# An FFN on the high parts of its weights, with a general path behind an If, on one Trainium2 core

## The chip, the cores and the metric

The kernel runs on one core of one Trainium2 chip. The metric is the device time of one execution in microseconds; less is better. Before the change the median of three runs is 2959.37 us (2954.0 to 2959.81).

## What is computed

The input x has 2 batches of 2048 tokens with 256 features, in float32. Cut to what matters:

```python
x = x + _layernorm(attn(_layernorm(x), Wq, bq, Wk, bk, Wv, bv, Wo, bo, gamma, beta))
x = x + _layernorm(ffn(_layernorm(x), w_gate, w_up, w_down))

# attn: 16 heads of 64, softmax over 2048 keys, then
#   y = x + attn_out; layer norm of y with eps 1e-3, times gamma, plus beta
# ffn: weights are int32 from -127 to 127, times SCALE = 1/127; HIDDEN is 768
gate = jnp.einsum('bsd,hd->bsh', x, wg)
up = jnp.einsum('bsd,hd->bsh', x, wu)
h = jax.nn.silu(gate) * up
return jnp.einsum('bsh,dh->bsd', h, wd)
```

## The kernel before

Products that must be more precise than the fast float32r format are made of two parts. A value is split into a high part (a cast to float32r) and a low part (what is left). A product then takes three matmuls: high by high, high by low, low by high.

**The attention** is 64 units (batch, pair of heads, block of 512 queries). It takes the first 2720 us. TensorE makes maxima of scores, scores and the product with V; ScalarE makes exponentials; VectorE and GpSimd add them up. Beside it, short jobs run in pieces: `piece` in `prep_jobs` (L328) loads 128x256 of integer weights, casts and transposes them, splits them into high and low parts and writes both to HBM; 18 of these jobs cover the three weights. `load_ffn` (L361) reads them back in the last units. `ahead_job` is the first of four `own_job`s (L393).

**The FFN** is written out by hand for PE, DVE, ACT and POOL; SP's order is left to the scheduler. Eight chunks of 512 tokens, six blocks of 128 hidden features each, make 48 slots, numbered 0 to 47 here. In each slot, `gate_up` (L968) issues on PE two accumulations of six matmuls, gp and up (128x512 each, two buffers each); on ACT the Silu of gp (`sg`, L984); on DVE `hf`, up times sg (L986); on ACT the cast to the high part of hT (L988); on POOL its low part (L989). After gate_up every job that is running makes one step, up to its next `yield`:

- `end_job` of the chunk before (L1037), started in a chunk's second slot: four output tiles (`down`, L992, 18 matmuls of 128x256 each; one tile, one tile, two tiles), their statistics, the reciprocal root (`ln_rstd`, L99: 13 small steps on DVE), then scale, residual add on POOL and output.
- `own_job`, for the four chunks of the second batch: three layer norms in a row on the attention's result, each with statistics (L96, L97), the 13 small steps, and two applies on ACT per step (L137), with adds and products on POOL (L416).
- `x_out` (L955): transposes of a chunk's normalized rows and their split.
- `last_units` (L1082): what is left of the attention.

Each engine works through its instructions in order: what stands in front of sg or hf on ACT or DVE delays it. Where each own_job starts is given by slot numbers:

```python
OWN_AT = {2: OWN + 1, 14: OWN + 2, 24: OWN + 3}
```

The intermediates of the 13 small steps lie in a PSUM bank (`chain`, L430). `finish` (L1053) makes the last chunk's four tiles and the final outputs.

Of the kernel before, what the change touches and what calls it, by code (L numbers as in the profile page):

```python
# [8 lines left out]
F32 = mybir.dt.float32  # L9
# [7 lines left out]
P = 128  # L17
# [8 lines left out]


@with_exitstack
def kernel(
    ctx: ExitStack,  # L30
# [15 lines left out]
    out: bass.AP,  # L46
):
    nc = tc.nc
    B, S, D = x.shape
# [27 lines left out]
    xT_dram = dram.tile([B, NC, P, 2, DC, TB], F32, name="xT_dram")  # L77
    wg_dram = dram.tile([P, 2, DC, HID], F32, name="wg_dram")
    wu_dram = dram.tile([P, 2, DC, HID], F32, name="wu_dram")
    wd_dram = dram.tile([P, 2, HC, D], F32, name="wd_dram")  # L80


    mvx = [const.tile([P, NT, 2], F32, name=f"mvx{b}") for b in range(B)]
    rsx = [const.tile([P, NT], F32, name=f"rsx{b}") for b in range(B)]
    nbx = [const.tile([P, NT], F32, name=f"nbx{b}") for b in range(B)]

    small["pool"] = st
# [10 lines left out]

    def ln_rstd(rs, nb, mv, n, eps, eng=None, bank=None):  # L99

        eng = eng or nc.vector

        def temp(k, name, dtype=F32):
            if bank is not None and name not in ("ng", "ny"):
                return bank[:, k * n : (k + 1) * n]
            return small["pool"].tile([P, n], dtype, tag=f"{name}{n}", name=name, bufs=2)

        v = temp(0, "nv")  # L110
        eng.tensor_scalar(v, mv[:, :, 1], eps, None, ALU.add)
        g = temp(1, "ng", I32)
        eng.tensor_scalar(g, v.bitcast(I32), -0.5, 1597463007.0, ALU.mult, ALU.add)

        def stt(out, a, s, b, op0):

            if eng is nc.vector:
                eng.scalar_tensor_tensor(out, a, s, b, op0, ALU.mult)
            else:
                eng.tensor_scalar(a, a, s, None, op0)  # L120
                eng.tensor_tensor(out, a, b, ALU.mult)

        h = temp(2, "nh")
        eng.tensor_scalar(h, v, -0.5, None, ALU.mult)
        y = g.bitcast(F32)
        for i in range(3):
            t = temp(3, "nt")
            eng.tensor_tensor(t, h, y, ALU.mult)
            t2 = temp(4, "nu")
            eng.tensor_tensor(t2, t, y, ALU.mult)  # L130
            d = rs if i == 2 else temp(5, "ny")
            stt(d, t2, 1.5, y, ALU.add)
            y = d
        stt(nb, mv[:, :, 0], -1.0, rs, ALU.mult)

# [192 lines left out]
    def prep_jobs():  # L328
        jobs = []

        def piece(w, dst, o, i0):
            src = hd.tile([P, TT, D], F32, tag="hx", name="wi")[:, 0, :].bitcast(I32)
            nc.sync.dma_start(out=src, in_=w[o * P : (o + 1) * P, i0 * P : (i0 + 2) * P])
            yield "R"
            f = hd.tile([P, TT, D], F32, tag="hy", name="wf")[:, 0, :]
            nc.scalar.copy(f, src)
            yield "F"
            ps = double()[:, 0, :]
            for i in range(2):
                nc.tensor.transpose(ps[:, i * P : (i + 1) * P], f[:, i * P : (i + 1) * P], ident)  # L340
            t = hd.tile([P, TT, D], F32, tag="ht", name="wt")[:, :2, :].bitcast(F32R)
            split(t, ps[:, : 2 * P])
            for k in range(2):
                nc.sync.dma_start(
                    out=dst[:, k, i0 : i0 + 2, o * P : (o + 1) * P],
                    in_=f32(t[:, k, :]).rearrange("p (i n) -> p i n", i=2),
                )

        for w, dst, no, ni in (
            (w_gate, wg_dram, HC, DC),  # L350
            (w_up, wu_dram, HC, DC),
            (w_down, wd_dram, DC, HC),
        ):
            for o in range(no):
                for i0 in range(0, ni, 2):
                    jobs.append(piece(w, dst, o, i0))
        return jobs
# [3 lines left out]
    def load_ffn(which):  # L361

        if which < 2:
            full = aw.tile([P, DC, S], F32R, tag=("xh", "xl")[which], name=f"fw{which}")
            full = full.rearrange("p c n -> p (c n)")
            n = 2 * DC * HID
            t = full[:, :n].rearrange("p (w c n) -> p w c n", w=2, c=DC)
            for w in range(2):
                for dc in range(DC):
                    nc.sync.dma_start(  # L370
                        out=f32(t[:, w, dc, :]), in_=(wg_dram, wu_dram)[which][:, w, dc, :]
                    )
                    yield None

            x0T[which] = full[:, n : n + DC * TB].rearrange("p (c n) -> p c n", c=DC)
            nc.sync.dma_start(out=f32(x0T[which]), in_=xT_dram[0, 0, :, which])
        else:
            i = 2 * (which - 2)
            t = kp.tile([P, 2, 2, D], F32R, tag="T1", name=f"fw{which}")
            for w in range(2):  # L380
                nc.sync.dma_start(out=f32(t[:, w]), in_=wd_dram[:, w, i : i + 2, :])
                yield None
        fwt[which] = t
# [9 lines left out]
    def own_job(ch):  # L393
# [5 lines left out]
        def norm(dst, src, eps, *then):  # L399
            pool = small["pool"]  # L400
            mv = pool.tile([P, TT, 2], F32, tag="mvh4", name="mvh")
            for n in range(0, TT, 2):
                ln_stats([src[:, n + i, :] for i in range(2)], mv, n)
                if n == 0:
                    yield
            rs = pool.tile([P, TT], F32, tag="rsh4", name="rsh")
            nb = pool.tile([P, TT], F32, tag="nbh4", name="nbh")
            ln_rstd(rs, nb, mv, TT, eps, *chain())
            for n in range(0, TT, 2):
# [19 lines left out]

    def chain():  # L430

        if "chain" in banks:
            return nc.vector, banks["chain"].tile([P, 512], F32, tag="c", name="chain")
        return nc.gpsimd, None
# [493 lines left out]
    banks["pool"] = ctx.enter_context(tc.tile_pool(name="ps_m", bufs=1, space=PSUM))  # L928
    banks["chain"] = ctx.enter_context(tc.tile_pool(name="ps_c", bufs=1, space=PSUM))
    fs = ctx.enter_context(tc.tile_pool(name="fs", bufs=2))  # L930
# [37 lines left out]
    def gate_up(ch, hc):  # L968
        gp = ps_g.tile([P, TB], F32, tag="g", name="gp")
        up = ps_g.tile([P, TB], F32, tag="u", name="up")  # L970
        for ps, w in ((gp, fwt[0]), (up, fwt[1])):
            n = 0
            for dc in range(DC):
                for wi, xi in ((0, 0), (0, 1), (1, 0)):
                    nc.tensor.matmul(  # L975
                        ps,
                        w[:, wi, dc, hc * P : (hc + 1) * P],
                        xTs[ch][xi][:, dc, :],
                        start=n == 0,
                        stop=n == 5,  # L980
                    )
                    n += 1
# [9 lines left out]
    def down(ch, i, hcs=range(HC)):  # L992
# [7 lines left out]
        for hc in hcs:  # L1000
            for n, (hi, wi) in enumerate(((0, 0), (0, 1), (1, 0))):
                nc.tensor.matmul(  # L1002
                    fp_tile(ch, i),
                    hTs[ch, hc][:, hi, i * P : (i + 1) * P],
                    fwt[2 + hc // 2][:, wi, hc % 2, :],
                    start=hc == 0 and n == 0,
                    stop=hc == HC - 1 and n == 2,
                )
# [6 lines left out]
    def end_stats(ch, i, mv):  # L1015
        ln_stats([fp_tile(ch, i)], mv, i)

    def end_rstd(mv):
        rs = small["pool"].tile([P, TT], F32, tag="rso", name="rso")
        nb = small["pool"].tile([P, TT], F32, tag="nbo", name="nbo")  # L1020
        ln_rstd(rs, nb, mv, TT, LN_EPS, *chain())
        return rs, nb

# [13 lines left out]
    def end_job(ch):  # L1037

        mv, before = end_mv(), ()
        for tiles in ((0,), (1,), (2, 3), ()):  # L1040
# [4 lines left out]
            before = tiles  # L1045
            if not tiles:
                ready = end_rstd(mv)
            yield
        end_out(ch, 0, *ready, nc.gpsimd)
        yield  # L1050
        end_out(ch, 2, *ready, nc.gpsimd)

    def finish(ch):  # L1053
# [3 lines left out]
        def end(tiles, eng):  # L1057
# [5 lines left out]
            nb = small["pool"].tile([P, n], F32, tag=f"nbe{n}", name="nbe")  # L1063
            ln_rstd(rs, nb, mv[:, :n, :], n, LN_EPS, *chain())
            yield
# [16 lines left out]
    def last_units():  # L1082

        wo_half(units[-2], 1)
        yield
        ps = bank()
        sum_up(last, ps)
# [7 lines left out]
        wo_half(last, 0)  # L1095
        yield
        yield
        wo_half(last, 1)

# [5 lines left out]
    end = len(chunks) - 1  # L1105
    OWN_AT = {2: OWN + 1, 14: OWN + 2, 24: OWN + 3}
    with tc.manual_schedule(engines={EV.PE, EV.DVE, EV.Activation, EV.Pool}):
        ffn_load(0)
        ffn_load(1)
        for ch in range(len(chunks)):  # L1110
            for hc in range(HC):
                gate_up(ch, hc)
                n = len(slots)
                if n == 0:
                    jobs.append(last_units())
                if n in OWN_AT:
                    jobs.append(own_job(OWN_AT[n]))
                if ch > 0 and hc == 1:
                    jobs.insert(0, end_job(ch - 1))
                if hc == 1 and OWN <= ch + 1 < len(chunks):  # L1120
                    jobs.append(x_out(ch + 1))
                for j in list(jobs):
# [5 lines left out]
        for j in jobs:  # L1128
            drain(j)
        finish(end)  # L1130


# [45 lines left out]
```

## Time and profile before

| what | value |
|---|---|
| runs, median of three | 2959.37 us |
| the profiled execution | 2961.08 us, its span 2959.3 us |
| mean granted TensorE clock | 0.992 |
| first gate_up on PE | 2724.71 us |
| hf of slot 0, of slot 46, of slot 47 | 2729.27, 2938.18, 2942.39 us |
| down in 2740 to 2960 us, x576 | busy 74.0 us |
| last vector add | 2955.84 us |

In the profile's rows an instruction reads: line, engine, operation, output from inputs, shapes, count, busy time in us, mean length in ns, then the engine's idle time just before and what ended it. "PE" is TensorE's matmuls, "PEld" its weight loads, "DVE" VectorE, "ACT" ScalarE, "POOL" GpSimd, "SP" the engine that issues most DMAs. Lengths of matmuls overlap; their rate is read from the chain, where a group's total is given. All times are from the span's start.

### The profile page before, as it was taken

To read this page: it belongs to the slowest core of one execution; us is meant where nothing else is said; L and a number is where in the kernel's file an instruction comes from. 1 tells how busy PE (TensorE), PEld (TensorE's weight loads), DVE (VectorE), ACT (ScalarE), POOL (GpSimd) and SP (SyncE) were. 2 spreads that over 40 slices of the span, in tenths; PEclk is the share of its full clock that TensorE was granted. 3 is DMA by queue.
4 is the path that set the end of the run, shared out by engine and by line. 5 is a ranking of instruction groups with operands and counts; after the bars stand their busy time and mean duration, and the time that the engine had idled before them with its cause. 6 is when DMAs were issued, how large, how long until landed. Compare 5 with 4: busy or idle time off the path is not lost.

```text
span 2959.3 us, 48771 instructions
## 1 busy us (share of the span) xinstructions
PE 2876.9 (97%) x19492; PEld 1742.6 (59%) x19492; DVE 2102.9 (71%) x2701; ACT 1467.1 (50%) x1740; POOL 2444.7 (83%) x1399
## 2 busy tenths in 40 slices
PE   7999999999999999989999999999999999999998
PEld 5555565556555565555655655555655555555787
DVE  6776677777777777766677767777677767774653
ACT  4545454544445444554455545555455445554443
POOL 4999878888788878877799989998799889888453
PEclk9999999999999999999999999999999999999999
DMA  2000000000000001010000001000000000012000
GB/s 59 19 12 11 14 12 12 12 15 5 17 10 14 9 12 31 5 35 10 26 21 10 7 10 33 5 20 24 5 6 24 21 1 31 23 58 72 29 29 29
DMA packets 125428, 59.14 MB, mean 20 GB/s; under 512 B 77232, under 2 KB 118448, under 8 KB 124816
## 3 DMA queue, kind: packets, MB, share of 16 engines
q1 hardware_dynamic: 124992, 55.62, 7.0%
q8 instruction: 152, 2.49, 0.4%
q0 software_dynamic: 208, 0.40, 0.1%
q14 instruction: 76, 0.62, 0.1%
HBM read 37.89 MB, written 17.83 MB: 19 GB/s over the span
## 4 chain that ended last, share of the span: by engine, by line
PE 85%; DVE 5%; POOL 4%; ACT 3%; issue 1%; DMA 1%; SPq 1%; ACTq 0%; DVEq 0%; POOLq 0%
PE t L670 32%; PE s L701 28%; PE s L626 8%; PE t L579 5%; PE t L604 3%; POOL accs L684 2%; ACT pt L671 2%; PE fp L1002 2%; PE s L199 2%; PE gp L975 2%; PE up L975 2%; PE t L253 2%; DVE two L688 1%; DVE nm L633 1%; DVE acc L264 1%
## 5 line engine op out<-in xcount | busy, mean ns | idle before, releaser
L684 POOL TENSOR_TENSOR accs<-accs,pt 128x1024 f32<-128x1024 f32 x636 | 1620.6, 2548 | 313.8 <-ACT pt L671 268.8
L633 DVE TENSOR_REDUCE nm<-s 128x2 f32<-128x1024 f32 x1024 | 1219.1, 1225 | 500.6 <-PE s L626 500.3
L671 ACT ACTIVATE pt<-t 128x1024 f32<-128x1024 f32 x1024 | 1049.8, 1027 | 184.7 <-PE t L670 117.8
L670 PE MATMUL t<-QN,KT 64*128 64x512 f32 x6144 | 916.0, 403 | 4.7 <-ACT pt L671 3.0
L701 PE MATMUL s<-pt,v 128*64 128x512 f32 x4096 | 908.1, 596 | 0.0
L670 PEld LDWEIGHTS t<-QN,KT 64*128 64x128 f32 x6144 | 521.2, 185 | 244.2 <-ACT pt L671 180.3
L701 PEld LDWEIGHTS s<-pt,v 128*64 128x64 f32 x4096 | 283.0, 137 | 538.4 <-issue 525.7
L626 PE MATMUL s<-KT,QN 64*128 64x512 f32 x2048 | 421.7, 408 | 5.6 <-DVE cf L230 4.1
L670 PE MATMUL t<-sh,unit 64*128 64x512 f32 x2048 | 405.8, 392 | 0.0
L691 POOL TENSOR_TENSOR accs<-accs,two 128x1024 f32<-128x1024 f32 x128 | 305.9, 2390 | 18.5 <-DVE two L690 7.5
L688 DVE TENSOR_TENSOR two<-pt 128x1024 f32<-128x1024 f32 x128 | 309.4, 2417 | 0.0
L223 ACT COPY rr<-s 128x1024 f32<-128x1024 f32 x63 | 63.9, 1015 | 430.2 <-PE s L199 417.0
L626 PEld LDWEIGHTS s<-KT,QN 64*128 64x128 f32 x2048 | 193.4, 185 | 108.4 <-issue 54.4
L649 ACT CAST sh<-t 128x512 fp32r<-128x512 f32 x64 | 37.6, 588 | 420.7 <-PE t L645 420.7
L670 PEld LDWEIGHTS t<-sh,unit 64*128 64x128 f32 x2048 | 192.9, 184 | 51.1 <-ACT sh L649 0.6
L264 DVE SCALAR_TENSOR_TENSOR acc<-t,rc,acc 128x256 f32<-128x256 f32 x500 | 206.9, 476 | 19.9 <-PE t L253 13.0
L579 PE MATMUL t<-xh,wqk 128*128 128x512 f32 x512 | 184.5, 421 | 18.2 <-ACT pt L671 10.5
L681 POOL TENSOR_TENSOR accs<-pt 128x1024 f32<-128x1024 f32 x64 | 154.9, 2420 | 0.5 <-ACT pt L671 0.5
L989 POOL TENSOR_TENSOR hT<-hf,hT 128x512 fp32r<-128x512 f32 x48 | 62.0, 1291 | 107.6 <-ACT hT L988 107.5
L579 PEld LDWEIGHTS t<-xh,wqk 128*128 128x128 f32 x512 | 99.6, 195 | 54.0 <-ACT pt L671 22.8
L589 ACT ACTIVATE QN<-t,bq_sb 128x512 fp32r<-128x512 f32 x64 | 44.1, 689 | 157.2 <-PE t L579 157.2
L253 PE MATMUL t<-wo,cs 64*128 64x256 f32 x1500 | 114.4, 285 | 2.0 <-ACT pt L671 1.8
(167 smaller groups left out, 2167.6 us busy)
## 6 DMA issues: line engine op xcount, KB each, us to landing
few<-rr SPq DMA_DIRECT2D x512, 0.5 KB, 2.0
xc<-in_L_attn_x_dram SPq DMA_DIRECT2D x8, 512.0 KB, 4.0
xT_dram<-hn SPq DMA_DIRECT2D x16, 256.0 KB, 2.1
out_dram<-o SPq DMA_DIRECT2D x14, 256.0 KB, 2.1
xT<-xT_dram SPq DMA_DIRECT2D x3, 1024.0 KB, 5.7
attn_dram<-acc SPq DMA_DIRECT2D x5, 512.0 KB, 2.6
acc<-in_L_attn_x_dram SPq DMA_DIRECT2D x4, 512.0 KB, 8.8
raw_w<-in_L_attn_Wq_dram SPq DMA_DIRECT2D x16, 128.0 KB, 2.2
```

The costliest lines, as they stand in the source:

```text
L253: nc.tensor.matmul(ps[e][:, i * D : (i + 1) * D], t[half(e), ci, s], w[half(e), wi, :], start=k == 0, stop=k == 2,)
L264: nc.vector.scalar_tensor_tensor(a, ps[e][:, i * D : (i + 1) * D], inv[:, e, q : q + 1], a, ALU.mult, ALU.add)
L579: nc.tensor.matmul(ps[:, k, :], w[:, wi, dc, :], xx[:, dc, s], start=n == 0, stop=n == 5)
L626: nc.tensor.matmul(s[:, e, :], QN[u][half(e), 0, qt * P : (qt + 1) * P], KT[b, p, kc][half(e), 0, :], start=True, stop=True,)
L633: nc.vector.tensor_reduce(nm[u][:, :, qt, kc : kc + 1], s, AX.X, ALU.max, negate=True)
L670: nc.tensor.matmul(ps[:, e, :], w, r, start=n == 0, stop=n == 3)
L671: nc.scalar.activation(pt, ps, AF.Exp, scale=QSCALE)
L681: nc.gpsimd.tensor_tensor(accs[u], todo[0], todo[1], ALU.add)
L684: nc.gpsimd.tensor_tensor(accs[u], accs[u], t, ALU.add)
L688: nc.vector.tensor_tensor(two, p8[n], p8[n + 1], ALU.add)
L691: nc.gpsimd.tensor_tensor(accs[u], accs[u], two, ALU.add)
L701: nc.tensor.matmul(pvs[u][half(e), 0, :], v[:, kt % 4, n : n + K], pt[:, e, :], start=kt % 8 == 0, stop=kt % 8 == 7,)
```

## The change

The kernel becomes two paths. The former kernel, changed, is `fast_path`. A second kernel with all parts, `general_path` (not shown: the same computation with split weights, 25447 instructions in all), stands behind an If.

- In the FFN the weights' low parts are left out: gate_up makes four matmuls for each of gp and up instead of six, a tile of down 12 instead of 18. Only high parts are written and read back.
- Each prep job takes the largest absolute value of its low part into a column of `wlow`. In slot 38 the job `verdict` makes one number of it, through a small DRAM row, and in slot 41 writes 1 to `good` where all are zero. After the fast path every engine loads `good` into a register; if it is below 1, general_path runs.
- The 13 small steps are issued in two parts, with a yield after the first six (`rstd_steps`). own_job has one more yield after the statistics. The own jobs start in slots 2, 10 and 16 instead of 2, 14 and 24, so that up to three run at a time. Each has its own statistics tiles and its own 32 columns of one lasting `chain` bank.
- x_out goes to the front of the list of jobs; two yields in last_units move.

```diff
-    def ln_rstd(rs, nb, mv, n, eps, eng=None, bank=None):
+    def ln_rstd(*a):
+        for _ in rstd_steps(*a):
+            pass
+
+    def rstd_steps(rs, nb, mv, n, eps, eng=None, bank=None, by=""):
...
             y = d
+            if i == 0:
+                yield
         stt(nb, mv[:, :, 0], -1.0, rs, ALU.mult)
...
-            split(t, ps[:, : 2 * P])
-            for k in range(2):
-                nc.sync.dma_start(
-                    out=dst[:, k, i0 : i0 + 2, o * P : (o + 1) * P],
-                    in_=f32(t[:, k, :]).rearrange("p (i n) -> p i n", i=2),
-                )
+            hi = t[:, :1, :].bitcast(F32R)[:, 0, :]
+            nc.scalar.copy(hi, ps[:, : 2 * P])
+            nc.vector.tensor_tensor(t[:, 1, :], ps[:, : 2 * P], f32(hi), ALU.subtract)
+            nc.vector.tensor_reduce(
+                wlow[:, k : k + 1], t[:, 1, :], AX.X, ALU.max, apply_absolute_value=True
+            )
+            nc.sync.dma_start(
+                out=dst[:, i0 : i0 + 2, o * P : (o + 1) * P],
+                in_=f32(hi).rearrange("p (i n) -> p i n", i=2),
+            )
...
-            for w in range(2):
-                for dc in range(DC):
-                    nc.sync.dma_start(
-                        out=f32(t[:, w, dc, :]), in_=(wg_dram, wu_dram)[which][:, w, dc, :]
-                    )
-                    yield None
+            for dc in range(DC):
+                nc.sync.dma_start(out=f32(t[:, dc, :]), in_=(wg_dram, wu_dram)[which][:, dc, :])
+                yield None
...
-            ln_rstd(rs, nb, mv, TT, eps, *chain())
+            yield from rstd_steps(rs, nb, mv, TT, eps, *chain(k), str(k))
...
-    def chain():
+    def chain(k):
 
         if "chain" in banks:
-            return nc.vector, banks["chain"].tile([P, 512], F32, tag="c", name="chain")
+            return nc.vector, banks["chain"][:, k * 32 : (k + 1) * 32]
         return nc.gpsimd, None
...
             for dc in range(DC):
-                for wi, xi in ((0, 0), (0, 1), (1, 0)):
+                for xi in range(2):
                     nc.tensor.matmul(
                         ps,
-                        w[:, wi, dc, hc * P : (hc + 1) * P],
+                        w[:, dc, hc * P : (hc + 1) * P],
                         xTs[ch][xi][:, dc, :],
...
-            for n, (hi, wi) in enumerate(((0, 0), (0, 1), (1, 0))):
+            for n in range(2):
                 nc.tensor.matmul(
                     fp_tile(ch, i),
-                    hTs[ch, hc][:, hi, i * P : (i + 1) * P],
-                    fwt[2 + hc // 2][:, wi, hc % 2, :],
+                    hTs[ch, hc][:, n, i * P : (i + 1) * P],
+                    fwt[2 + hc // 2][:, hc % 2, :],
...
-            if not tiles:
-                ready = end_rstd(mv)
-            yield
-        end_out(ch, 0, *ready, nc.gpsimd)
+            if tiles:
+                yield
+        rs = small["pool"].tile([P, TT], F32, tag="rso", name="rso")
+        nb = small["pool"].tile([P, TT], F32, tag="nbo", name="nbo")
+        yield from rstd_steps(rs, nb, mv, TT, LN_EPS, *chain(4), "o")
         yield
-        end_out(ch, 2, *ready, nc.gpsimd)
+        end_out(ch, 0, rs, nb, nc.gpsimd)
+        yield
+        end_out(ch, 2, rs, nb, nc.gpsimd)
...
+    def verdict():
+
+        t = op.tile([P, 4], F32, tag="few", name="ok")
+        nc.vector.tensor_reduce(t[:, 1:2], wlow, AX.X, ALU.max)
+        nc.vector.tensor_scalar(t[:, 1:2], t[:, 1:2], 0.0, None, ALU.is_equal)
+        nc.sync.dma_start(out=ok_dram.rearrange("(p o) -> p o", o=1), in_=t[:, 1:2])
+        row = op.tile([1, P], F32, tag="cf", name="row")
+        nc.sync.dma_start(out=row, in_=ok_dram.rearrange("(o n) -> o n", o=1))
+        yield
+        yield
+        yield
+        nc.vector.tensor_reduce(t[0:1, 3:4], row, AX.X, ALU.min)
+        nc.vector.tensor_copy(good, t[0:1, 3:4])
...
-    OWN_AT = {2: OWN + 1, 14: OWN + 2, 24: OWN + 3}
+    OWN_AT = {2: OWN + 1, 10: OWN + 2, 16: OWN + 3}
...
+                if n == 38:
+                    jobs.append(verdict())
...
-                    jobs.append(x_out(ch + 1))
+                    jobs.insert(0, x_out(ch + 1))
...
+def tile_attn_ffn_sandwich_kernel(tc: tile.TileContext, *args):
+    nc = tc.nc
+    with tc.tile_pool(name="good", bufs=1) as pool:
+        good = pool.tile([1, 1], I32, name="good")
+        fast_path(tc, *args, good)
+        value = nc.values_load(good[0:1, 0:1], min_val=0, max_val=1)
+        with tc.If(value < 1):
+            general_path(tc, *args)
```

## The prediction

> **What bounds the kernel now.** I read the busy row of the page first, then the busy times by stretch, because the change works on one stage only.
>
> ```profile
> PE 2876.9 (97%) x19492; PEld 1742.6 (59%) x19492; DVE 2102.9 (71%) x2701; ACT 1467.1 (50%) x1740; POOL 2444.7 (83%) x1399
> ...
> PEclk9999999999999999999999999999999999999999
> ```
>
> PE sets the end almost everywhere, at its full clock. The last stage (the FFN) looks less tight. From 2740 us, columns PE, PEld, DVE, ACT, POOL (busy us and instructions), then PEclk, DMA share and GB/s:
>
> ```profile
> 2740.00:2760.00 20.00, 13.94 (x76) 10.86 (x75) 15.99 (x62) 8.40 (x16) 12.55 (x10) 0.87 0.00 0
> 2760.00:2780.00 20.00, 20.00 (x116) 17.88 (x116) 8.81 (x36) 8.84 (x16) 7.70 (x6) 0.95 0.01 1
> 2780.00:2800.00 20.00, 20.00 (x124) 17.87 (x123) 13.31 (x57) 8.87 (x17) 8.96 (x7) 1.00 0.33 106
> ```
>
> PE is full but for one hole, and DVE is at a half to four fifths. Who waits for whom in 2720 to 2960 us, and the price of each step there (busy us, mean ns):
>
> ```profile
> POOL hT L989 <- ACT hT L988: 107.5, 41, 5.8
> ACT hT L988 <- DVE hf L986: 87.1, 48, 6.2
> DVE hf L986 <- PE up L975: 47.4, 17, 5.8
> ...
> DVE hf L986 <- ACT sg L984: 25.0, 11, 3.1
> ```
>
> ```profile
> L986 DVE SCALAR_TENSOR_TENSOR hf<-up,sg 128x512 f32<-128x512 f32 x48 | 33.1, 690 | 75.2 <-PE up L975 47.4 <-ACT sg L984 25.0 <-issue 1.6
> L988 ACT CAST hT<-hf 128x512 fp32r<-128x512 f32 x48 | 29.8, 621 | 87.1 <-DVE hf L986 87.1
> L984 ACT ACTIVATE sg<-gp 128x512 f32<-128x512 f32 x48 | 28.4, 592 | 33.9 <-PE gp L975 33.9
> L118 DVE SCALAR_TENSOR_TENSOR nbo<-mvo,rso 128x4 f32<-128x4 f32 x7 | 2.2, 316 | 0.2
> ```
>
> hf waits for PE 47 us in all, but already 25 us for ACT. So a second limit stands close behind PE. The chain of the work that ended last (start, length, what) shows PE's rates without a gap:
>
> ```profile
> 2822.38 4.27 PE fp L1002 x36
> 2826.65 1.39 PE gp L975 x6
> 2828.03 1.37 PE up L975 x6
> 2829.41 1.37 PE gp L975 x6
> ```
>
> Six 512-column products take 1.37 us (0.229 each), 36 of 256 columns 4.27 us (0.119 each).
>
> **PE's share of the change.** Each slot (one gate_up) drops 4 of 12 products, 4 x 0.229 = 0.91 us; 48 slots make 43.9 us. Each of 32 output tiles drops 6 of 18, 6 x 0.119 = 0.71 us, 22.7 us in all. PE loses 66.6 us. Its order is otherwise unchanged, and up to the FFN it is the same instruction for instruction.
>
> **The second limit.** DVE and ACT work in order. In a slot DVE does hf and then the jobs' small steps; ACT does sg, hT and then the jobs' applies. The next slot's sg stands behind those applies on ACT, the next hf needs that sg. So from one hf to the next passes at least the larger of (a) all DVE work of the slot, and (b) hf plus all ACT work of the slot. From the timeline, start to start: hf 0.69, sg 0.50, hT 0.55, one apply 0.50, a bn_stats with its aggregate 0.54, a small step on four columns 0.18 (13 of them make a 2.36 us chain), 0.12 for the hand-overs. Check: hf at 2811.21 and 2814.05 with two applies between, 2.84; sum 0.69 + 0.55 + 1.00 + 0.50 + 0.12 = 2.86.
> I made both sums for every slot from the two programs' orders. One slot of after as a sample, slot 10, the fifth of chunk 1 (on PE only eight products, 1.83): hf, the output's two statistics and half chain, a job's two statistics, another job's half chain, a third's two statistics: 0.69 + 6 x 0.54 + 12 x 0.18 = 6.1 us. From hf of slot 0 to hf of slot 46, by chunk 0 to 7 (the last one's first four slots):
> - before, PE: 18.8, 25.9, 25.0, 25.9, 25.9, 25.9, 25.9, 19.5, sum 192.8. DVE/ACT: 21.6, 27.3, 21.9, 23.5, 24.5, 23.1, 16.5, 8.4, sum 167.0. Larger by chunk 197.1, larger by slot 223.0. Measured (hf at 2729.27 and 2938.18): 208.9.
> - after, PE: 13.3, 17.6, 16.7, 17.6, 17.6, 17.6, 17.6, 13.0, sum 130.8. DVE/ACT: 19.7, 25.5, 27.1, 25.8, 22.3, 17.4, 16.3, 9.4, sum 163.6. Larger by chunk 168.6, by slot 180.0.
> PE may run two slots ahead (two gp and two up buffers), so the truth lies between the two: before, (208.9 - 197.1) / (223.0 - 197.1) = 0.46 of the way. The same share of after's gap: 168.6 + 0.46 x 11.4 = 173.8. The jobs' steps are not fewer, only spread: they, not PE, become the bound in chunks 0 to 4. POOL's sums per chunk (at most 14 steps of 1.3, 18.2) stay below.
>
> [...] Each chain ends in a step that reads two SBUF tiles (nbh, nbo). Row: nbo takes 316 ns on the mean against 161 for its neighbours, one of them 1.25 us while POOL worked, with POOL busy about half of the stage. [...] I take the row, 2 us more: 175.8. Gain of the stage 208.9 - 175.8 = 33.1 us.
>
> **The rest, in order.**
> - The end: in before hf of slot 46 to the end is 21.1 us. After, hf of slot 47 comes 0.4 us earlier in this count, the product of tile 2 is 12 instead of 18 long: 0.9 us less.
> - The look at the low parts: 18 reduces of 128x256 on DVE. Not in the trace; nearest row, bn_stats of 128x256, 0.40 us, so 7.2 us of work. They stand after the subtract of a weight piece, where DVE next idles (7.38 us idle before the following max in the unit at 325 us). Cost between 0 and 7.2; I take 0.3, as they lie in that idle time. Half the weight writes and reads go from SP's queue, which binds nothing: 0.
> - The verdict, slots 38 to 41: four small DVE steps (about 0.8 us, in slots where PE is the longer) and two DMAs in series, 2 x 2.1 us plus issues. It waits three slots (over 8 us), so DVE finds the row there. SP's register load waits for it; behind it on SP are only the outputs of chunk 5 on, which come at slot 42. 0.
> - The If: every engine loads one register and jumps over the general path. No row shows a jump over code; nearest, instruction fetches are DMAs (228 packets for 3.11 MB), and a 128 KB DMA lands in 1.7 us. [...] I take 2.2; bounds 0 and 6, no gain since nothing is removed there.
> Sum: -33.1 - 0.9 + 0.3 + 2.2 = -31.5. Against the profiled execution (2961.08, span 2959.3) 2929.6; against the median of the runs, 1.7 lower, 2927.9. I give 2928.0.
>
> **Rivals.**
> 1. PE stays the bound (the loop of DVE and ACT hidden by the two-slot lead): 192.8 - 130.8 = 62 off, about 2959.4 - 62 - 0.9 + 2.5 = 2899. For: PE is full in most stretches. Against: 25 us of hf's waits are already for ACT. 4 in 100.
> 2. [...] 18 in 100.
> 3. Slower: the TensorE clock falls. One hole of 5.54 us (PE waits for acc) left 0.87 in its 20 us. In after PE is idle for about a quarter of the stage. At half clock all through it needs 2 x 130.8 = 261.6, 52.7 more than 208.9: 3014. It decides from a mean clock of 130.8 / 208.9 = 0.63 on. Against: holes of over 4 us come only in some six slots. 4 in 100.
> 4. The low parts are not all zero, and the general path runs as well: integers up to 127 fit, so hardly; it would add another pass, about 2900 us. 1 in 100.
> The forecast with its own spread (2914 to 2938): 73 in 100. The range, with the bounds of If, lock and lead, is 2914 to 2946: it leaves out rivals 1, 3 and 4 and half of 2, 18 in 100. A measurement here can tell 0.2% (5.9 us) from no change; of rival 2 I put 1 in 100 there. So faster 0.94, same 0.01, slower 0.05.
>
> **What would show it.** hf of slot 46 about 176 us after the first; PE busy near 131 us of it; hf waiting for sg and not for up in chunks 1 to 4; slots 10, 11, 16 and 17 at 5.5 to 6.3 us; nbo and nbh at most 0.4 us; 1 to 3 us of nothing after the last output. If hf still waits for up mostly, or a row of PEclk under 0.8 stands in the stage, a step is wrong.

## The result and the profile after

After the change the median of seven runs is 2946.88 us (2943.49 to 2948.64); seven runs of the kernel before have 2960.28 us. The ratio is 0.9952, interval 0.994 to 0.9964: about 13 us faster, less than half of the 31.5 forecast, and just above the forecast's range. The profiled execution took 2943.49 us (span 2941.5), 17.8 us less than that of before in span. Where these 17.8 us are:

| stretch | before | after | forecast of the difference | measured |
|---|---|---|---|---|
| start to hf(0) | 2729.27 | 2725.86 | 0.3 | -3.4 |
| hf(0) to hf(46) | 208.9 | 192.8 | -33.1 | **-16.1** |
| hf(46) to the end of the last vector add | 18.1 | 17.5 | -0.9 | -0.6 |
| from there to the end | 3.0 | 5.3 | 2.2 | +2.3 |

The end and the If came as forecast; the first row mostly moves by itself (below). The miss is the second row, from hf(0) to hf(46), called the stage here. The busy row and the clock row of the page:

```profile
PE 2825.7 (96%) x19108; PEld 1693.3 (58%) x19108; DVE 2116.3 (72%) x2723; ACT 1466.2 (50%) x1740; POOL 2443.0 (83%) x1399
...
PEclk9999999999999999999999999999999999999889
```

The last three slices, the FFN, fall from 9 to 8. The busy times by stretch (PE, PEld, DVE, ACT, POOL, then PEclk, DMA share, GB/s) for the same stretches as before, and one more:

```profile
2740.00:2760.00 20.00, 14.19 (x71) 10.91 (x70) 13.25 (x51) 8.14 (x16) 11.43 (x10) 0.74 0.03 1
2760.00:2780.00 20.00, 13.57 (x74) 11.11 (x72) 16.47 (x69) 5.80 (x11) 9.32 (x8) 0.92 0.15 53
2780.00:2800.00 20.00, 17.84 (x90) 15.77 (x91) 13.35 (x51) 13.40 (x26) 16.55 (x13) 0.82 0.20 54
2800.00:2820.00 20.00, 11.85 (x58) 9.88 (x58) 15.08 (x65) 9.10 (x18) 7.19 (x6) 0.74 0.16 44
```

PE, full in two of three such rows before, is now full in none. From 2760 to 2780 it is busy 13.57 of 20 us, and at a lower clock; DVE has 16.47. Who waits for whom in 2720 to 2925 us:

```profile
ACT hT L1803 <- DVE hf L1801: 83.3, 47, 5.0
POOL hT L1804 <- ACT hT L1803: 79.7, 37, 4.8
DVE hf L1801 <- ACT sg L1799: 28.6, 15, 5.9
...
PE fp L1817 <- ACT o L950: 24.1, 6, 6.5
DVE hf L1801 <- PE up L1790: 20.6, 9, 5.0
```

hf's waits for PE fell from 47.4 to 20.6 us, those for ACT's sg stand at 28.6 (25.0 before), and in chunks 1 to 4 it is 15.8 us for sg and 3.1 for up, as forecast. A wait is new: PE's `down` for ACT's `o`, 24.1 us in six waits. In before it was 0.4 us. Then the steps themselves:

```profile
L1801 DVE SCALAR_TENSOR_TENSOR hf<-up,sg 128x512 f32<-128x512 f32 x48 | 33.2, 691 | 51.4 <-ACT sg L1799 28.6 <-PE up L1790 20.6 <-POOL hT L1804 1.6
...
L929 DVE SCALAR_TENSOR_TENSOR nbo<-mvo,rso 128x4 f32<-128x4 f32 x7 | 6.5, 924 | 0.2
L929 DVE SCALAR_TENSOR_TENSOR nbh<-mvh,rsh 128x4 f32<-128x4 f32 x11 | 5.0, 457 | 0.4
```

nbo, a step on four columns, now takes 924 ns on the mean (316 before), nbh 457 (209 before); the forecast had put both at 0.4 us at most. And the chain of the work that ended last: its shares by line over the stage (the start of each row), first before, then after:

```profile
by line: PE fp L1002 25.5%; PE gp L975 23.0%; PE up L975 22.4%; issue 4.9%; DVE hf L986 3.7%; ACT acc L137 2.5%; DVE bs L96 2.2%; PE misc L962 2.0%; ACT o L137 1.9%; DVE chain L128 1.6%; DVE chain L130 1.6%; ACT sg L984 1.2%; POOL accs L691
```

```profile
by line: PE fp L1817 14.4%; PE gp L1790 9.9%; PE up L1790 9.1%; DVE hf L1801 8.0%; issue 6.4%; DVE bs L902 5.0%; DMA ok_dram<-ok 3.9%; ACT acc L950 3.7%; ACT o L950 3.6%; POOL acc L1230 2.6%; DVE chain L941 2.6%; SPq L1021 2.4%; DVE chain L
```

The three groups of PE's products were 71% of it and are 33% now. A piece of it in after:

```profile
2850.78 0.32 issue
2851.10 0.59 ACT acc L950
2851.69 0.49 ACT sg L1799
...
2852.26 0.69 DVE hf L1801
2852.95 0.35 DVE bs L902
2853.33 0.18 DVE mvo L903
```

An apply of a job on ACT, behind it sg, behind it hf, behind it the statistics: the loop that the forecast had as "second limit". So the bound moved towards DVE and ACT, as foreseen; but the stage is 192.8, above the forecast's larger sum, by slot, of 180.0.

### The profile page after: what moved, and what is told of

Its sections match the earlier page's. It is cut to its first block, busy times and chain, and to the rows that moved or that the text cites. A ratio compares the mean times of both kernels' runs of the same rounds, so it can differ in the third digit from the quotient of the medians.

```text
span 2941.5 us, 48043 instructions
## 1 busy us (share of the span) xinstructions
PE 2825.7 (96%) x19108; PEld 1693.3 (58%) x19108; DVE 2116.3 (72%) x2723; ACT 1466.2 (50%) x1740; POOL 2443.0 (83%) x1399
## 4 chain that ended last, share of the span: by engine, by line
PE 83%; DVE 6%; POOL 4%; ACT 3%; issue 1%; DMA 1%; SPq 1%; ACTq 0%; DVEq 0%; POOLq 0%
PE t L1484 32%; PE s L1515 28%; PE s L1440 8%; PE t L1393 5%; PE t L1418 3%; POOL accs L1498 2%; ACT pt L1485 2%; PE s L1012 2%; PE t L1066 2%; DVE two L1502 1%; PE fp L1817 1%; DVE nm L1447 1%; DVE acc L1077 1%; PE t L1459 1%; PE gp L1790 1%
## 5 line engine op out<-in xcount | busy, mean ns | idle before, releaser
L1393 PE MATMUL t<-xh,wqk 128*128 128x512 f32 x512 | 183.1, 418 | 18.0 <-ACT pt L1485 10.5
```

Source lines behind the costliest of these rows:

```text
L1393: nc.tensor.matmul(ps[:, k, :], w[:, wi, dc, :], xx[:, dc, s], start=n == 0, stop=n == 5)
```

## The experiments

Theory A when they began: the loop of DVE and ACT binds slot by slot, and the new order, which splits the output's chain of roots, frees the banks of fp one slot later, so that PE loses its two-slot lead at each chunk's `down`; two waits in chunk 0 were added to it later. Rivals: PE's lower granted clock (theory C); the cut and the order each help, or the general path costs all through. "By slot" is the sum, over the 46 slots, of the larger of PE's and the loop's time, worked out for each order as in the prediction; these sums are estimates, good to some 2 us. Each stage is read from one profile per kernel.

**The cut alone**, and **the order alone**, each put into before (the diff is of the cut; that of the order is the diff of the change without the products, weights, verdict and If):

```
-                for wi, xi in ((0, 0), (0, 1), (1, 0)):
+                for wi, xi in ((0, 0), (0, 1)):
...
-            for n, (hi, wi) in enumerate(((0, 0), (0, 1), (1, 0))):
+            for n, (hi, wi) in enumerate(((0, 0), (1, 0))):
```

> Before, with only the products of the low weights left out (gate_up 8 instead of 12, down 2 per block instead of 3; the low parts are still made and loaded, and the order of all else, the whole chains and the old slots of the jobs stay; no If). Numbers from the slot sums: PE 130.8, loop of DVE and ACT 167.0, larger by chunk 172.6, by slot 186.4 us from hf(0) to hf(46), against 208.9 measured before. Theory A (the slot loop binds, and after loses PE's two-slot lead because its output chain is split and frees the banks of fp one slot later): here the banks come free as before, so the lead stays and the stage lies inside its two sums, 173 to 186: the time is 2960.3 minus 23 to 36, about 2930, that is some 15 us faster than after. Theory B (the loop binds by the slot, and the new order is what makes it shorter): 186.4 plus the 13 us that after has above its slot sum, about 199: 2950. Theory C (PE's lower granted clock binds, not the order): as after without its If, 2944.

> Before, with only the new order (chains in two parts, own jobs at slots 2, 10 and 16, x_out ahead, the last attention unit's steps moved, one lasting chain bank, end_job's output a slot later), and all 12 and 18 products; no If. Slot sums: PE 192.8, loop 163.6, larger by chunk 195.8, by slot 216.6, against 197.1 and 223.0 of before. Theory A (the split delays the banks of fp and PE loses its lead): the stage goes from 208.9 to the slot sum 216.6 or beyond: 4 to 12 us slower than before, 2964 to 2972. Theory B (the order is what makes the loop shorter): 0.46 of the way between the sums as before, 205.4: 3.5 us faster, 2957. Theory C (clock): PE is full in both, nothing changes, 2960.

The cut alone took 2933.42 us, ratio 0.991 (0.9895 to 0.9925), its stage 182.9: 26.5 us faster than before. The order alone took 2976.17, ratio 1.0056 (1.0042 to 1.007), its stage 226.6: 16 us slower. Theory A was the nearest to both, and too small for the second (4 to 12 us were expected). With the If's 2.7 us (next), cut and order would add up to 2952.3; measured is 2946.9. So the change consists of a cut worth 26.5 us, an order that takes about 11 of it back, and the If.

**Without the If**, and **the output's chain whole** (two edits of after):

```
-        value = nc.values_load(good[0:1, 0:1], min_val=0, max_val=1)
-        with tc.If(value < 1):
-            general_path(tc, *args)
...
-        yield from rstd_steps(rs, nb, mv, TT, LN_EPS, *chain(4), "o")
+        ln_rstd(rs, nb, mv, TT, LN_EPS, *chain(4), "o")
```

> After without the register load, the If and the general path behind it (the look at the low parts and the verdict's row stay). From the last vector add to the end after has 5.75 us where before has 3.46. If this is the price of the load and the jump, the time is 2.3 us less than after, 2944.6, and the end stands 3.4 to 3.6 us behind the last add. If the If's price is only in these 2.3 us, the stage from hf(0) to hf(46) stays at 193 within 1 us; a rival, that the larger program also makes instruction fetches slower all through, would give more than 4 us less.

> After, with the output job's root chain in one part again (its step of 13 small operations stands in one slot, and the output's applies come one slot earlier). Theory A (late release of the banks of fp: PE waits 24.1 us for ACT's o in 6 waits): these waits fall under 8 us in all and the time is 4 to 8 us less than after, 2939 to 2943. Theory B (only the sums of the slots count): the sums by slot rise by the half chain that meets two statistics more, 0 to 3 us more than after. Theory C (clock): the holes of PE are shorter, its mean clock in the stage rises by over 0.05 and the time falls by 4 us or more; the granted clock of the windows and the hf of slots with no wait for o tell it from A.

Without the If: 2944.23 us, 2.65 less, which the medians alone don't tell from nothing; the stage is 192.67 against 192.78; the rest after the last add is 3.1 us (the 5.75 and 3.46 of the expectation count from that add's start). The price is at the end and nowhere else. What is there shows in the DMA queues from 2936 us, the last add, to the end (packets, MB, share):

```profile
q14 instruction: 8, 0.07, 4.7%
```

Without the If this row is missing from the same stretch: eight more packets of instructions are fetched. SP's branch starts at 2936.71 us, and its next instruction at 2939.27; the packets lie between 2936.6 and 2940.2. That fits a fetch after the branch; whether the fetch alone makes the price isn't shown. With the If the end took 5.3 to 6.7 us in twelve of the profiles here, without it 3.0 to 3.1 in four: 2.3 to 3.7 us, and it varies.

The output's chain whole: 2943.13, 3.7 less; its stage 187.7, 5.1 less. Here too the medians' intervals overlap, and the stage and the waits do the telling. PE's waits for ACT's o fell from 24.1 to 2.8 us. The timeline of after around slot 43 shows the mechanism (start, length, engine, what, idle time before and who ended it):

```profile
2903.30 1.02 ACT L950 ACTIVATE o<-fp,nbo,rso 128x256 f32<-128x256 f32 x2
...
2904.37 2.93 PE L1817 MATMUL fp<-fw,hT 128*128 128x256 f32 x12 [3.05 <-ACT o L950]
...
2907.09 1.91 PE L1790 MATMUL gp<-xT,fw 128*128 128x512 f32 x4
2908.80 1.69 PE L1790 MATMUL up<-xT,fw 128*128 128x512 f32 x4
...
2910.62 0.69 DVE L1801 SCALAR_TENSOR_TENSOR hf<-up,sg 128x512 f32<-128x512 f32 x1 [5.04 <-PE up L1790]
```

`down` needs the bank that o still reads, and waits 3.05 us; gp and up of the next slots are queued behind it on PE, and after the hole they run at 1.91 and 1.69 us per four products where 1.10 is the rate. hf finds up missing by 5.04 us. The granted clock there, before PEclk come busy times as above:

```profile
2903.27:2910.10 6.83, 5.73 (x20) 5.06 (x21) 0.69 (x1) 3.67 (x8) 5.03 (x4) 0.50 0.18 58
```

With the chain whole, the same place:

```profile
2901.02 1.70 PE L1817 MATMUL fp<-fw,hT 128*128 128x256 f32 x12 [0.37 <-ACT o L950]
...
2902.56 1.10 PE L1790 MATMUL gp<-xT,fw 128*128 128x512 f32 x4
2903.50 1.10 PE L1790 MATMUL up<-xT,fw 128*128 128x512 f32 x4
```

The slot fell from 5.73 to 1.93 us. Two things had lengthened it: the hole, and behind it the half clock, at which these three groups take 6.1 us from the first start to the last end, against 3.6. But slots 10, 16 and 22 grew (10 from 5.89 to 7.30), where the whole chain meets other jobs' statistics; that is a part of why 21 us of waits gave only 5. The edit also shortens nbo: its mean fell from 924 to 260 ns, 4.7 us in all, while nbh rose by 0.8. So the 5.1 us aren't the price of the late banks alone.

**The old order with cut and If** (the order's part of the diff undone), and **chunk 0** (the chain on GpSimd, to which the program gives no bank, whole; the inverse a slot later):

```
-            if i == 0:
+            if i == 0 and bank is not None:
                 yield
...
         yield
+        yield
         inv_item(last)
-        yield
         wo_half(last, 0)
```

> After in the order of before: whole chains, own jobs at slots 2, 14 and 24, x_out last among the jobs, the last attention unit's steps and end_job as before; the cut, the look at the low parts, the verdict and the If stay. If the parts add (the cut alone 2933.4, the If 2.7, the look and the halved weight loads 0.3 less what they save on DMA), 2935 to 2937, and hf(0) to hf(46) is 183 us as with the cut alone, with its waits: PE for ACT's o under 6 us, misc for xT about 11. A rival: the low parts' loads or the reduces, which only this one has beside the old order, cost the 10 us that lie between the cut alone and after; then 2944 to 2947.

> After, with two edits in chunk 0: the ahead job's chain on GpSimd in one part again, and the last unit's inverse one slot later, together with the first half of its output product. Theory A (in chunk 0 after loses 3.7 us in slot 1, where the ACT applies wait 3.6 us for POOL's nbh behind hT(0), and 2.4 us in slot 4, where DVE's rc waits 2.7 us for the DMA of few): both waits go, chunk 0 falls from 26.4 to 20 to 22 us, and the time is 4 to 6 us less, 2941 to 2943. Theory B (the slots only take it up again later, since PE's lead rules): chunk 0 falls but the sum falls by under 2 us. Theory C: chunk 0 is bound by the acc of the attention's last units, which this does not touch: no change.

The old order: 2935.69 us, ratio 0.9915 (0.9902 to 0.9929), stage 183.6. The parts add: the look at the low parts and their smaller loads cost nothing that shows, and the new order costs 11.2 us of time, 9.2 of stage. One thing that differs in the stage beside the waits: nbo and nbh take 4.5 us in all here and 11.5 in after. Chunk 0's two edits: 2939.77, 7.1 less; stage 186.6, chunk 0 from 26.4 to 22.7, and both waits are gone. Slot 1 of after had shown the first:

```profile
2731.35 0.19 POOL L939 TENSOR_TENSOR nt<-nh,ny 128x4 f32<-128x4 f32 x1
...
2733.83 0.20 POOL L932 TENSOR_TENSOR nbh<-mvh,rsh 128x4 f32<-128x4 f32 x1
...
2734.06 1.09 ACT L950 ACTIVATE acc<-acc,nbh,rsh 128x256 f32<-128x256 f32 x2 [3.57 <-POOL nbh L932]
2735.06 0.57 ACT L1799 ACTIVATE sg<-gp 128x512 f32<-128x512 f32 x1
...
2735.73 0.69 DVE L1801 SCALAR_TENSOR_TENSOR hf<-up,sg 128x512 f32<-128x512 f32 x1 [5.89 <-ACT sg L1799]
```

The split moved the second half of GpSimd's chain behind hT(0) on POOL; the applies on ACT wait for its last step, and sg, which is ready, stands behind the applies.

**Old starts of the own jobs** in after:

```
-    OWN_AT = {2: OWN + 1, 10: OWN + 2, 16: OWN + 3}
+    OWN_AT = {2: OWN + 1, 14: OWN + 2, 24: OWN + 3}
```

> After, with the own jobs started at slots 2, 14 and 24 again; chains stay split. Slot sums 178.8 against 180.0 of after. Compared with the cut alone, after loses 6.0 us in chunk 2 and 2.6 in chunk 3 and wins 3.0 and 3.6 back in chunks 4 and 5. Theory A (the late banks of fp, on the output's chain, cost in every chunk): chunks 2 and 3 give 2 to 4 us, chunks 4 and 5 take as much, 0 to 3 us less than after in all. Theory B (three chunks' jobs side by side is the cost): 6 us or more less than after, under 2941.

2940.16 us, 6.7 less; stage 189.2, only 3.6 less (chunks 1 to 3 gave 7.5 us, 4 to 6 took 3.8). With split chains an own job lasts 17 slots in place of 11, so the last of these jobs isn't over at slot 37, where x_out reads its rows: one chunk goes into the FFN before its last normalization. So it isn't a version to use; it says that three jobs side by side are not free, but 3.6 and 6.7 lie between the two theories and decide neither.

**sg ahead**: the next slot's gate_up and sg are issued ahead of this slot's hf, hT (in `hidden`) and jobs.

```
+        gate_up(0, 0)
...
-                gate_up(ch, hc)
                 n = len(slots)
+                if n + 1 < len(chunks) * HC:
+                    gate_up((n + 1) // HC, (n + 1) % HC)
+                hidden(ch, hc)
```

> After, with the next slot's gate_up and sg issued ahead of this slot's hf, hT and jobs: sg stands no longer behind the applies on ACT, and PE's next gate_up no longer behind a down that waits for a bank. Slot sums: the larger of DVE, ACT and PE 162.3 in place of 180.0. Theory A (the loop hf, hT, applies, sg, hf and the blocked PE lead set the time): the stage falls from 192.8 by 10 to 20 us, the time to 2927 to 2937, and hf's waits for sg fall from 28.6 to under 10 us. Theory C (clock): PE has as many holes, so its clock stays low and the time falls by under 4 us. Theory D: the banks of gp and up are held one slot longer, and PE waits for hf instead: 0 to 5 us slower than after.

2917.85 us, ratio 0.9854 (0.9839 to 0.9869): 29 us less than after, stage 165.3. This supports theory A, which had expected 10 to 20 us less stage; 27.5 came. The edit moves PE's products and ACT's sg together, so it doesn't tell which of the two frees more. Its waits:

```profile
POOL hT L1808 <- ACT hT L1807: 55.5, 27, 4.8
ACT hT L1807 <- DVE hf L1805: 46.7, 22, 5.3
ACT sg L1799 <- PE gp L1790: 27.3, 22, 3.6
```

hf is hardly the one that waits any more (4.1 us for sg, under 2 for up); DVE is busy 116.5 of the 165.3 us.

**PE's work put back**, in after, and the combinations:

```
-            for dc, xi in ((0, 0), (0, 1), (1, 0), (1, 1)):
+            for dc, xi in ((0, 0), (0, 0), (0, 0), (0, 1), (1, 0), (1, 1)):
```

> After with PE's work of before in gate_up put back: each accumulator takes 6 products, the first of them three times over (so the hidden values are not those of the reference; the amount of work is what counts). It adds 4 x 0.229 = 0.91 us to each slot, 42 us to hf(46): PE 172.8, loop 163.6, by slot 196.5 against 180.0. Theory A (each slot takes the longer of PE and the loop, since PE's lead is lost): 14 to 18 us more than after, 2961 to 2965, that is nothing is left of the cut in gate_up although PE then has 20 us to spare. Theory B (the loop of DVE and ACT alone sets the time, PE has two slots of lead): 0 to 5 us more. Theory C (clock: after's PE runs at 0.74 to 0.9 in many windows because it is idle, and that costs): with PE fuller the clock rises above 0.95 in the windows of chunks 1 to 4, and the time is less than by A, 2950 to 2957.

> After in the order of before (2935.7 with that alone), and with the next slot's gate_up and sg ahead of this slot's hf, hT and jobs (2917.9 in the new order). Slot sums of the larger of DVE, ACT and PE: 167.4 here, 162.3 in the new order. Theory A (with sg ahead the slot sums hold, and the price of the split order, 11 us, was the lost lead that sg ahead gives back): 3 to 8 us slower than the new order with sg ahead, 2921 to 2926. Theory B (the split order costs its 11 us whatever the order of sg): 2905 to 2910.

> After with sg ahead (2917.9), and the two edits of chunk 0 (GpSimd's chain whole, the last unit's inverse a slot later with the first half of its product), which gave 7.1 us in the order of after. Slot sums 162.9 against 162.3. Theory A (the two waits of chunk 0 are DMA and POOL latencies that no order of sg hides): 4 to 7 us less, 2911 to 2914. Theory B (they were the same loss that sg ahead takes away): within 2 us of 2917.9.

> After with the output's chain whole (3.7 us less by itself) and the two edits of chunk 0 (7.1 less by itself). If they are separate places, 10.8 us less, 2936, which is what the whole old order gives (2935.7). If the waits of chunk 0 only come back as waits for the banks (PE for ACT's o grew from 24.1 to 27.8 us with the edits of chunk 0), the sum is more than the parts: under 2934. If they overlap: 2939 to 2941.

PE's work put back: 2961.29 us, ratio to before 1.0005 (0.9996 to 1.0014), stage 207.0. By its slot sum 14 to 18 were expected, 14.4 came. This speaks against the clock as the main cause (theory C): over the stage the granted clock rose from 0.87 to 0.93, and the time did not fall below theory A's. More telling is that the order alone, at a clock of 0.95, stands 10 us above its sum, and the old order with the cut, at 0.91, stands 3 below. The run also shows that after has little spare time on PE where it counts: 42 us of work beside its idle 40 us cost 14.

In the old order with sg ahead: 2918.33, the new order with it 2917.85; the stage is 163.0 against 165.3. So sg ahead gives back what the split had cost (theory B is out by 8 us). By the slot sums the old order should have been 3 us slower at least; the stage says no, while the ratios to before, 0.9865 and 0.9854 from separate sets of runs, can't tell. sg ahead and chunk 0: 2916.75, 1.1 less in time as theory B has it, 3.8 in the stage: most of what these edits gave had been given back before.

Chain whole and chunk 0 together: 2935.57, stage 183.7: as the old order. So undoing these two takes back all that the new order cost; in time they add (3.7 and 7.1 alone, 11.3 together), in the stage less so (5.1 and 6.2 alone, 9.1 together).

**Means and variances in PSUM**, in after and in the version with sg ahead and chunk 0:

```
-            mv = pool.tile([P, TT, 2], F32, tag=f"mvh{k}", name="mvh", bufs=1)
+            mv = chain(k)[1][:, 24:32].rearrange("p (t n) -> p t n", n=2)
```

> After with the means and variances of the chains on DVE in the chain's PSUM bank, so that the last step of a chain (nbo, nbh) reads one tile of SBUF in place of two. In after nbo takes 924 ns on the mean (7 times) and nbh 457 (11 times), against 316 and 209 before and 161 for the small steps next to them: 6.5 + 5.0 us, of which 18 x 0.16 = 2.9 are the work. Theory A (these 8.6 us are DVE standing still while POOL works, and they lie in the slots where DVE is the longer: 17, 23, 29, 35, 41 each 0.6 above the sum): nbo and nbh fall to about 0.2 us and the time is 3 to 6 us less than after, 2941 to 2944. Theory B (PE's late start of down is what these slots wait for): the steps shorten, the time stays within 2 us of 2946.9. Theory C (the length is not from the second tile of SBUF): nbo stays at 0.9 us.

> After with sg ahead, the two edits of chunk 0 (2916.8 with these) and the means and variances in PSUM. With sg ahead DVE's sum by slot is the longer one in chunks 1 to 4, so by theory A of the run before each shorter nbo or nbh counts: 3 to 6 us less, 2911 to 2914. By theory B nothing, 2915 to 2918.

In after: 2937.76 us, 9.1 less, more than theory A's 3 to 6; the stage 186.8, 6.0 less. The two rows:

```profile
L929 DVE SCALAR_TENSOR_TENSOR nbh<-chain,rsh 128x4 f32<-128x4 f32 x11 | 1.8, 161 | 0.4
L929 DVE SCALAR_TENSOR_TENSOR nbo<-chain,rso 128x4 f32<-128x4 f32 x7 | 1.1, 161 | 0.2
```

Both have the length of their neighbours, so the excess (8.6 us) came with the second SBUF tile, and removing it shortened the stage by 6.0. With all edits: 2912.51 us, ratio 0.9844 (0.983 to 0.9857), stage 158.4. That is the fastest version here, 34 us less than after.

Stages beside their sums by slot, where a sum was worked out:

| kernel | time, us | sum by slot | stage | stage less sum |
|---|---|---|---|---|
| before | 2960.3 | 223.0 | 208.9 | -14.1 |
| cut alone, old order | 2933.4 | 186.4 | 182.9 | -3.5 |
| cut, If, old order | 2935.7 | 186.4 | 183.6 | -2.8 |
| order alone | 2976.2 | 216.6 | 226.6 | +10.0 |
| after | 2946.9 | 180.0 | 192.8 | **+12.8** |
| after, old starts of the own jobs | 2940.2 | 178.8 | 189.2 | +10.4 |
| after, PE's work put back | 2961.3 | 196.5 | 207.0 | +10.5 |
| after, chain whole and chunk 0 | 2935.6 | 184.1 | 183.7 | -0.4 |
| after, sg ahead | 2917.9 | 162.3 | 165.3 | +3.0 |
| old order, sg ahead | 2918.3 | 167.4 | 163.0 | -4.4 |

In this table the kernels with the whole split order and without sg ahead stand 10 to 13 us above their sums; the old order, and the split with its two places undone, stand below. Not in it is the split order with one thing mended (chunk 0, the chain whole, or the means in PSUM): the stages are 186.6 to 187.7, by estimate some 5 to 8 us above their sums of 180 to 183.

## Why the prediction was right in part, and where it failed

- **PE's share** was right in amount and in that the bound moves to DVE and ACT. PE was busy 152 us of the stage instead of the forecast's 131; 131 at the stage's mean clock of 0.87 makes 150. This slowing is real (PEclk 0.74 in two rows, the sign that the forecast had named for a wrong step). The clock is halved (0.50 granted) for 51 us of the stage in eight stretches, each of which begins in a hole of PE of 2.1 us or more or at most 2.5 us behind it. So the holes come first; but the half clock makes each dearer (some 2.5 us in slot 43), which no sum here contains. How much it adds over the stage wasn't measured.
- **The loop's price per slot** was right: slots 10, 11, 16 and 17 took 5.89, 6.11, 6.01 and 6.09 us, forecast 5.5 to 6.3.
- **The step that failed**: "PE may run two slots ahead (two gp and two up buffers), so the truth lies between the two ... The same share of after's gap: 168.6 + 0.46 x 11.4 = 173.8." Even where only the cut is made the share is not 0.46 but (182.9 - 172.6) / (186.4 - 172.6) = 0.75: 4 us. And the split order puts the stage outside of the two sums altogether: 12.8 us above the larger. The lead of PE hangs not on gp and up alone, but also on the banks of fp, which the forecast did not follow: their last reader, o, comes a slot later when the chain is split. PE's waits for o show it: 0.4 us before, 24.1 in after, 2.8 with the chain whole.
- **The order** was counted as spreading the same steps ("not fewer, only spread"). By the forecast's rule that is a gain: with the cut alone, 172.6 by chunk and 186.4 by slot, 172.6 + 0.46 x 13.8 = 178.9; with the order too, 173.8, so 5.1 less stage. It cost 9.2 of stage, 11.2 of time. This term of the wrong sign, 14.3 us, is most of the 17.0 by which the stage missed its 175.8; the rest is 4.7 of the old order with the cut (183.6 against 178.9), less the 2 allowed for nbo and nbh. Undoing two places takes it back (9.1 of stage, 11.3 of time): the output's split chain, with its late banks and its longer nbo, and chunk 0, where POOL's chain behind hT(0) and the DMA of `few` (waits of 3.6 and 2.7 us) were not in the sums.
- **The longer nbo and nbh** ("lock" in the forecast's range) were taken as 2 us. No run shows that figure; it was the author's estimate from the row of before, where nbo takes 316 and nbh 209 ns against 161: 7 x 0.155 + 11 x 0.048 = 1.6 us. In after the excess is 8.6 us, and the run with the means and variances in PSUM makes it 6.0 in the stage. There such a step, with one SBUF input, takes 161 ns in each of 18 cases. With two, its length differs with the order: nbo 924 ns in after, 310 in the old order with the same cut. What lengthens it wasn't shown.
- **The If**: no run shows the 2.2 us of the sum, the author's estimate; measured are 2.3 in the profiles and 2.65 by the medians. SP's next instruction begins 2.6 us after its branch (2936.71 to 2939.27 us), and eight more packets of instructions arrive behind the last add. **The tail and the reduces**: -0.6 (forecast -0.9), and nothing that shows.
- **The verdict** cost 0.2 us of DVE's time, but by luck: its two DMAs were taken as 2.1 us each, the first landed after 7.5 us and both took 10.7 of the 11 us that the slots left. In the kernels with sg ahead, whose slots are shorter, DVE waits 1.0 to 3.2 us for that row.
- Nearest came the upper end of the range, 2946, which stands for no use of the lead. That much held: as an estimate, 192.8 less the excess of nbo and nbh (6.0) and chunk 0 (6.2), each measured by itself, leaves 180.6 us of stage, and the sum by slot is 180.0. That the time came so close is in part luck: the range allowed 6 for the If, another estimate, where 2.3 came, and had nothing for chunk 0 (6.2) and the start (-3.4).

Open: how the price of the split divides exactly, since the places overlap (chain whole 5.1, chunk 0 6.2, nbo and nbh 6.0 us of stage, together more than the 12.8; the whole chain shortens nbo as well, so the late banks by themselves weren't measured), what the half clock adds, and what the side-by-side jobs cost by themselves.

## What to carry to other kernels

When work is cut from the engine that binds, price not only the next engine's sums but each buffer that the first engine waits for, by its last reader: a step that is split or deferred holds its bank a slot longer, and everything queued behind that wait is late (here PE's waits for o grew from 0.4 to 24.1 us). A new order can also come with longer small steps (nbo here 316 and 924 ns): compare their mean lengths before and after. In a loop that passes through three in-order engines, issue the next turn's first steps ahead of this turn's side jobs; here that was worth about as much (29 us) as the cut of a third of the products (26.5). A change of work and a change of order in one edit are best run apart: here one gained and the other lost.

## What the runs showed that was not expected

- The stage repeats to 0.1 us from after to its twin without the If (192.78 and 192.67; one profile each), while hf(0) lies anywhere from 2723.3 to 2730.6 us in the profiles, with nearly the same work before it. If that pair is typical, the stage tells edits apart that the medians of five runs blur.
- After a hole of 3.05 us PE's twelve products of down took 2.93 us in place of 1.6 to 1.7, and the next fours 1.91 and 1.69 in place of 1.10: 6.8 us at a granted clock of 0.50.
- Passing over this If, whose body never runs here, costs 2.3 to 3.7 us at the end, and nothing that shows elsewhere.
